# Four stacked graph layers on one core: layer 3 reordered, small VectorE steps moved, and the order of all chains from a table

## The chip, the cores and the metric

The kernel runs on one NeuronCore of a Trainium2 chip. The metric is the device time of one execution in microseconds (us). A core has engines that run side by side, each with its own queue that is worked off in order: PE (TensorE) multiplies 128x128 blocks and writes only to PSUM, DVE (VectorE) and POOL (GpSimd) do elementwise work, ACT (ScalarE) evaluates functions and copies, and SP (SyncE) issues DMAs between HBM and the on-chip memory SBUF. Engines wait for each other through semaphores. Three executions of the kernel before took 1044.95, 1046.66 and 1048.72 us; the median is 1046.66 us.

## The reference, cut to what matters

Inputs are x (32 batches of 512 nodes with 128 features, float32), one adjacency matrix adj (512x512, zeros and ones) and the weights. Every layer normalizes x over the features, takes the positive part, and adds the result of its own graph layer to x.

```
def layer(x, graph):
    h = maximum(layernorm(x), 0)
    return x + graph(h, adj)

# layer 0: h = x @ Wo;  u1 = h @ a1;  u2 = h @ a2
#   e = leaky(u1[idx1] + u2[idx2], 0.1)   (fixed pairs of nodes)
#   att = softmax(where(adj > 0, e, -9e15), over the FIRST index)
#   out = att @ h + x @ Ws
# layer 1: h = x @ Wp + bp;  s = leaky(src_i + dst_j, 0.2), softmax over j where adj > 0
#   h_gat = relu(layernorm((attn * adj) @ h))
#   z = relu(layernorm(((1 + eps) * h_gat + adj @ h_gat) @ W1 + b1))
#   out = relu(z @ W2 + b2 + h_gat)
# layer 2: Wh = h @ W;  e = leaky(f1_i + f2_j, 0.2), softmax over j where adj > 0
#   out = elu(att @ Wh + bias)
# layer 3: h0 = x @ W[0];  h1 = x @ W[1]
#   A = softmax over j of values drawn from e at the edges (the same for every batch)
#   out = (A * I) @ h0 + (A * (1 - I)) @ h1 + bias
```

Layer 3 needs, for each batch, the diagonal of A times h0 and the rest of A times h1. The product A x W can be multiplied in either order.

## The kernel before, in words

**Tiles.** A batch of 512 nodes is four chunks of 128 nodes on 128 partitions; a tile is 128x(4x128) float32. PSUM is eight banks of that size. Everything is float32; a 128x128 by 128x128 product is issued as two matmul passes.

**Preparation.** Once per execution, `prepare` and `prepare_last` load the weights and build what all batches share: `bias` (the mask, NEG where there is no edge), `adjT` (adj transposed), `biasT` (the mask transposed, first half, for layer 0), `edgeT` (0.2 times the mask transposed, for layer 2), `adjTe`, and for layer 3 `offT` (A without its diagonal, transposed) and `adiag_rep` (the diagonal, in every partition).

**One chain for each layer and batch** (`layer0` to `layer3`), 128 in all. Each begins with `preln`: VectorE takes mean and variance (L544, L546), 1/deviation comes from Ln and Exp on ScalarE (L560, L564) or from a power on GpSimd (L579), and the normalization itself runs on ScalarE for the first nine batches of layer 0 (L599) and on GpSimd otherwise (L614), four instructions of 128x128 each. Four transposes on TensorE (L454) put it into PSUM as `pt`, and ScalarE takes the positive part into `hT` (L624).

- Layer 0 projects `hT` with `w0_ext`, which has 128 weight columns and two score columns (L649), and copies the result out (L445). VectorE adds the two score columns (`sc`, L772) and takes the leaky ReLU (`ls`, L776); TensorE repeats `ls` along the free dimension (`prow`, L454). The scores of node pairs come from a matmul for the first nine batches (L749) and from small DMAs for the others (L759); `lt` is their leaky ReLU, on ScalarE for the first nine (L808) and on VectorE for the others (L801, L810). Then masked maxima (L791), exponentials (L848), and the products (L905 to L918).
- Layer 1 projects, adds a scalar to the scores (`src`, L939), attends (L672 to L726), squares the softmax sums for the layer norm (`q`, L950), multiplies by the adjacency (`pg`, L976: four blocks of 128x512), and runs a two-layer perceptron (L635).
- Layer 2 attends with rows and columns exchanged (L1021 to L1040); its mask is added by GpSimd (L1026).
- Layer 3 multiplies `hT` by the weights first (`p1`, L635: four 128x128 products), copies that to `h1` (L445), scales `pt` by the diagonal with the positive part taken (`own`, L1076), and for each of four output chunks accumulates `own` times W[0] (L1087) and four products of `offT` with `h1` (L1091). VectorE adds x and the bias (L1098) and SP writes the batch out.

**The order.** `Plan` writes the program's order by hand before anything runs. Every operation has an estimated length and a due time, `turn = begin + STRETCH * way`, where `begin` is that of its chain, `way` the length of the longest path to it within the chain, and STRETCH is 5.94. The begin of a chain is the sum of the gaps of the chains before it (GAPS, one for each layer; the first six gaps are widened by RAMP). The chains are listed with layer 1, 2 and 3 lagging layer 0 by 5, 11 and 16 batches (LAGS). The preparation has due times of its own (PREPARED, FILLED: a first one and a step). `run` then takes, again and again, the operation that could begin first on its engine by the estimates, and among those that could begin within SLACK of each other the one with the earliest due time, as long as its chain is among the WINDOW oldest unfinished ones and a tile is free. So an engine's queue is one fixed list; an operation whose input is late holds up all behind it on that engine. Where the plan sees TensorE idle for over 0.6 us, it puts in transposes that nobody reads (`idle`, L362). GpSimd operations are held by an added dependency behind VectorE operations that read through the same port.

Of the kernel before, what the change touches and what calls it, by code (L numbers as in the profile page):

```python
# [37 lines left out]
P = 128  # L38
NEG = -9.0e15
# [3 lines left out]
WINDOW = 24  # L43

OLD, KEPT = 1, 0
# [3 lines left out]
RESERVE = 1  # L49
# [13 lines left out]
SLACK = 0.112  # L63

STRETCH = 5.94

PREPARED, FILLED = (15.9, 2.63), (122.8, 2.7)

RAMP = 3.87
# [3 lines left out]
EARLY = 9  # L73

GAPS, LAGS = (2.58, 26.51, 19.83, 4.4), (0, 5, 11, 16)
# [32 lines left out]
class Operation:  # L108
    def __init__(self, engine, length, emit, chain, slots):
        self.engine, self.length, self.emit, self.chain, self.slots = engine, length, emit, chain, slots  # L110
        self.after, self.missing = [], 0
        self.ready = 0.0
        self.load, self.transfers, self.port = 0.0, 0, 0
        self.way = 0.0


class Plan:
# [4 lines left out]
    def __init__(self, tc):  # L122
        self.tc = tc
        self.ops = []
        self.chains = []
        self.begin = 0.0
        self.banks, self.idle_products = None, None

    def chain(self, gap=0.0, beside=None, name=""):


        self.chains.append([0, beside, self.begin, name])
        self.begin += gap

    def op(self, engine, length, emit, reads=(), writes=(), load=0.0, transfers=0, port=0):
# [3 lines left out]
        op.load, op.transfers, op.port = load, transfers, port  # L139
# [12 lines left out]
        for n in needs:  # L152
            n.after.append(op)
            if n.chain == k:
                op.way = max(op.way, n.way + n.length + DELAY[n.engine])
        count, beside, begin, _ = self.chains[k]
        turn = begin + STRETCH * op.way if beside is None else beside[0] + beside[1] * count
# [5 lines left out]
    def run(self):  # L163
# [18 lines left out]
        for _ in range(len(self.ops)):  # L182
# [59 lines left out]
            done = end + DELAY[op.engine]  # L242
# [39 lines left out]
def kernel(  # L282
# [36 lines left out]
    assert F == P and C == 4 and NE % P == 0 and AHEAD <= B <= 2 * HELD  # L319
# [35 lines left out]

# [38 lines left out]
    att = const("att", (P, 2))  # L394
# [11 lines left out]
    biasT = const("biasT", (P, C, N2))  # L406
# [11 lines left out]
    w0_ext = const("w0_ext", (P, P2))  # L418
# [40 lines left out]
    def score_weights(w, v_w, a_cols, v_a, cols, v_cols):  # L459
# [5 lines left out]
        op(PE, 0.15, lambda: nc.tensor.matmul(pc.t[:, 0, 0:2], lhsT=wT.t[:, 0, :], rhs=a_cols, start=True, stop=True),  # L465
           [wT, v_a], [pc])
        copy_op(DVE, 0.1, lambda: cols, lambda: pc.t[:, 0, 0:2], [pc], [v_cols])
# [6 lines left out]
    load(lambda: att, l0_att.rearrange("(t p) o -> p (t o)", p=P), [v_att])  # L474
# [6 lines left out]
    score_weights(lambda: wt_o.t[:, 0, :], wt_o, att, v_att, w0_ext[:, P:P2], v_w0)  # L481
# [26 lines left out]
    def no_edges():  # L508

        nc.vector.tensor_copy(cnt2T, counts.t[:, :, 1])  # L510
        nc.vector.tensor_scalar(maxbT, cnt2T, 0.0, NEG, ALU.is_le, ALU.mult)
# [6 lines left out]
    def mask_first():  # L518
        for jb in range(C):
            nc.vector.tensor_scalar(biasT[:, jb, :], adjT[:, jb, 0:N2], 0.0, NEG, ALU.is_le, ALU.mult)  # L520
# [63 lines left out]
    def preln(b, engine):  # L584
# [3 lines left out]
        rstd = inv_dev(mv, POOL if engine is ACT else ACT)  # L588
        shift = Value()
        xn = value(by_act if engine is ACT else by_pool, "xn")  # L590
        if engine is ACT:
# [5 lines left out]
            def norm():  # L597
                for c in range(C):
                    nc.scalar.activation(  # L599
                        xn.t[:, c, :], src[:, c, :], AF.Identity, bias=shift.own[:, c : c + 1],  # L600
# [21 lines left out]
        turn_op(lambda k: pt.t[:, k, :], lambda k: xn.t[:, k, :], [xn], [pt])  # L622
        hT = value(by_act, "hT")
# [16 lines left out]
    def project_scored(hT, w_ext, reads, first=0):  # L640

        h = parts(scored, "h", 2)
        for k in range(2):
            pt = value(banks, "proj")

            def emit(k=k, pt=pt):
                p = pt.t.rearrange("p (c t) f -> p c (t f)", c=2)[:, :, 0:P2]
# [5 lines left out]
                ACT, 0.26, lambda k=k: h[k].t[:, 2 * k : 2 * k + 2, first : first + P2],  # L653
                lambda pt=pt: pt.t.rearrange("p (c t) f -> p c (t f)", c=2)[:, :, 0:P2], [pt], [h[k]],
# [9 lines left out]
    def masked_max(prow, src, v_src, out, writes):  # L664

        rmax, top = Value(), [Value() for _ in range(C)]
        for ib in range(C):
# [9 lines left out]
            op(DVE, 0.61, emit, [prow, v_bias], [*writes(ib), top[ib]])  # L677
# [7 lines left out]
        def emit_nmax():  # L685
            nmax.own = small("nmax")
# [51 lines left out]
    def layer0(b):  # L738
        hT, _ = preln(b, ACT if b < EARLY else POOL)
        if b + AHEAD < B:  # L740
            load_x(b + AHEAD)
        h = project_scored(hT, w0_ext, [v_w0, v_w0b])
# [25 lines left out]
        sc, ls = Value(), Value()  # L768

        def emit_sc():  # L770
            sc.own = small("sc")
            nc.vector.tensor_add(sc.own, h[0].t[:, :, P], h[0].t[:, :, P + 1])  # L772

        def emit_ls():
            ls.own = small("ls")
            nc.vector.scalar_tensor_tensor(ls.own, sc.own, 0.1, sc.own, ALU.mult, ALU.max)  # L776

        dve(0.08, emit_sc, h, [sc], port=1)
        dve(0.08, emit_ls, [sc], [ls], port=1)
# [3 lines left out]
        for hf in range(H):  # L783

            def emit_max(hf=hf):
# [3 lines left out]
                for k in range(2):  # L789
                    jb = 2 * hf + k  # L790
                    nc.vector.tensor_tensor_reduce(  # L791
                        wide(y[hf].t)[:, k * N2 : k * N2 + N2], node[:, hf, :], biasT[:, jb, :], 1.0, LOWEST,
# [10 lines left out]
        def emit_lt():  # L803
            lt.own = small("lt", (P, 2, H))
            sums = u.sums.t[:, 0, 0:H] if early else lt1.own
            lt1_2 = sums.rearrange("p (o h) -> p o h", o=1).to_broadcast([P, 2, H])
            if early:
                nc.scalar.activation(lt.own, lt1_2, AF.Prelu, alpha=0.1)  # L808
                return
            nc.vector.scalar_tensor_tensor(lt.own, lt1_2, 0.1, lt1_2, ALU.mult, ALU.max)  # L810
# [13 lines left out]
        if early:  # L824
            op(ACT, 0.12, emit_lt, [u.sums], [lt])
        else:
            dve(0.08, emit_lt1, [u], [lt1], port=1)
            dve(0.08, emit_lt, [lt1], [lt], port=1)
# [103 lines left out]
    def layer1(b):  # L932
# [4 lines left out]
        def emit_src():  # L937
            src.own = small("src")
            nc.vector.tensor_add(src.own, h[0].t[:, :, P], score_p.to_broadcast([P, C]))  # L939

        dve(0.08, emit_src, [*h, v_score_p], [src], port=1)
# [6 lines left out]
        def emit_q():  # L948
            q.own = small("q")
            nc.vector.scalar_tensor_tensor(q.own, ssum[0].own, LN_EPS, ssum[0].own, ALU.mult, ALU.mult)  # L950
# [523 lines left out]
```

## Time and profile before

| | |
|---|---|
| three executions, median | 1046.66 us (1044.95 to 1048.72) |
| the profiled execution's own time | 1045.94 us |
| its span, first to last instruction | 1044.2 us |
| granted TensorE clock, mean | 0.998 |
| busy: TensorE matmul / weight load | 97% / 89% |
| busy: VectorE / ScalarE / GpSimd | 91% / 75% / 69% |
| TensorE passes / idle transposes among them | 8192 / 51 |

The page of the profile gives busy time for each engine (PE is the matmul, PEld the weight load that overlaps it), the span in 40 slices, the chain of work that ended last, and groups of instructions by source line with their count, busy time, mean duration and the idle time before them. Instructions of one engine overlap in their records: a matmul pass of 128 columns is on record for 275 ns, but passes of a stream start about 111 ns apart. The view by windows gives the busy time of each engine in a stretch of the span with the number of instructions, the timeline lists merged instructions by start, and the view of waits adds up who waited for whom.

The batches run through the layers like a pipeline: layer 0 of all batches is done after about 805 us of the span, layer 1 after about 925, layer 2 after about 1022; the first batch of layer 3 is added up (L1098) at 334 us and the last at 1040.

### The profile page before, as it was taken

How to read it: one execution, taken by the hardware profiler on the slowest of the kernel's cores; microseconds unless marked ns; L12 is line 12 of the kernel's file. 1: busy time of each engine (PE TensorE's matmuls, PEld its weight loads, DVE VectorE, ACT ScalarE, POOL GpSimd, SP SyncE). 2: the span in 40 equal slices, each digit the busy share in tenths (PEclk: the TensorE clock that was granted, in tenths of full speed). 3: DMA queues.
4: the chain of work that ended last, by engine and by line, in shares of the span. 5: the costliest groups of instructions: out<-in, count | busy, mean ns of one | idle time of the engine just before them, and what ended most of it. 6: DMA issues, size and time to landing. Idle time of an engine off the chain costs nothing.

```text
span 1044.2 us, 24575 instructions
## 1 busy us (share of the span) xinstructions
PE 1016.9 (97%) x8192; PEld 928.3 (89%) x8192; DVE 952.2 (91%) x3814; ACT 787.8 (75%) x2210; POOL 724.7 (69%) x962
## 2 busy tenths in 40 slices
PE   7999999999999999999999998999999999999998
PEld 6997888888899998989998898888989898899998
DVE  7999999999999999999999999999999988878862
ACT  7989787887887887777877776777777777766651
POOL 4563554786776767668767667767677677788992
PEclk9999999999999999999999999999999999999999
DMA  7300000000000000000000000000000000000011
GB/s 220 82 2 1 2 1 12 12 11 11 2 12 21 12 12 21 21 22 11 12 5 8 12 12 11 2 11 12 12 11 12 12 11 12 12 11 22 22 31 41
DMA packets 51726, 20.44 MB, mean 20 GB/s; under 512 B 16400, under 2 KB 51088, under 8 KB 51600
## 3 DMA queue, kind: packets, MB, share of 16 engines
q1 hardware_dynamic: 51600, 18.87, 6.9%
q8 instruction: 65, 1.06, 0.4%
q14 instruction: 61, 0.50, 0.2%
HBM read 10.43 MB, written 8.39 MB: 18 GB/s over the span
## 4 chain that ended last, share of the span: by engine, by line
PE 51%; DVE 36%; ACT 7%; POOL 4%; issue 2%; DMA 0%; SPq 0%; DVEq 0%; POOLq 0%; ACTq 0%
PE pt L454 7%; PE po L726 7%; PE pg L976 7%; PE po L1091 5%; DVE st L544 5%; PE po L1040 5%; DVE cols L1028 4%; PE proj L649 4%; PE prow L454 4%; DVE y L672 4%; DVE unused L672 3%; PE po L908 2%; DVE pT L721 2%; DVE mv L546 2%; DVE hn L964 2%; ACT y L705 2%
## 5 line engine op out<-in xcount | busy, mean ns | idle before, releaser
L614 POOL TENSOR_SCALAR xn<-xs,shift,rstd 128x128 f32<-128x128 f32 x476 | 232.6, 503 | 27.1 <-PE pt L454 19.4
L1026 POOL TENSOR_TENSOR cols<-cols,edgeT 128x512 f32<-128x512 f32 x128 | 161.4, 1278 | 69.5 <-ACT cols L1021 49.1
L1091 PE MATMUL po<-h,offT 128*128 128x128 f32 x1024 | 135.4, 275 | 0.5 <-ACT h L445 0.5
L976 PE MATMUL pg<-adjTe,hg 128*128 128x512 f32 x256 | 131.2, 595 | 1.0 <-ACT hg L971 0.9
L1091 PEld LDWEIGHTS po<-h,offT 128*128 128x128 f32 x1024 | 124.6, 192 | 0.7 <-ACT h L445 0.7
L1040 PE MATMUL po<-h,cols 128*128 128x129 f32 x1024 | 122.5, 275 | 0.0
L726 PE MATMUL po<-h,pT 128*128 128x128 f32 x1024 | 120.8, 275 | 0.1
L1040 PEld LDWEIGHTS po<-h,cols 128*128 128x128 f32 x1024 | 118.3, 192 | 0.7 <-issue 0.4
L726 PEld LDWEIGHTS po<-h,pT 128*128 128x128 f32 x1024 | 117.4, 192 | 0.7 <-ACT h L445 0.2
L544 DVE BATCH_NORM_STATS2 st<-xs 128x6 f32<-128x128 f32 x512 | 109.9, 276 | 6.7 <-POOL xs L1069 3.6
L649 PEld LDWEIGHTS proj<-w_ext,hT 128*128 128x128 f32 x768 | 94.9, 191 | 14.5 <-ACT hT L624 8.5
L649 PE MATMUL proj<-w_ext,hT 128*128 128x130 f32 x768 | 104.4, 277 | 2.5 <-ACT hT L624 2.0
L713 ACT ACTIVATE y<-y,nmax 128x512 f32<-128x512 f32 x128 | 90.7, 713 | 7.9 <-DVE nmax L687 4.7
L624 ACT ACTIVATE hT<-pt 128x512 f32<-128x512 f32 x128 | 74.7, 596 | 28.3 <-PE pt L454 19.8
L1030 ACT ACTIVATE cols<-cols 128x512 f32<-128x512 f32 x128 | 78.4, 634 | 22.2 <-DVE cols L1028 21.9
L1028 DVE TENSOR_TENSOR cols<-cols,prow 128x512 f32<-128x512 f32 x128 | 82.6, 678 | 13.7 <-PE prow L454 7.8
L672 DVE CUSTOM_DVE_ANT_0 unused<-prow,bias 128x512 bf16<-128x512 f32 x128 | 88.1, 688 | 6.3 <-PE prow L454 3.7
L705 ACT ACTIVATE y<-y,src 128x512 f32<-128x512 f32 x128 | 82.9, 712 | 13.6 <-DVE src L939 11.2
L721 DVE TENSOR_TENSOR pT<-pt,adjT 128x512 f32<-128x512 f32 x128 | 82.5, 683 | 9.6 <-PE pt L454 8.7
L1021 ACT ACTIVATE cols<-prow,h 128x512 f32<-128x512 f32 x128 | 80.1, 684 | 10.2 <-PE prow L454 10.1
L672 DVE CUSTOM_DVE_ANT_0 y<-prow,bias 128x512 f32<-128x512 f32 x128 | 82.2, 681 | 0.0
L454 PEld LDWEIGHTS pt<-ident,y 128*128 128x128 f32 x512 | 58.0, 141 | 26.5 <-ACT y L713 12.7
(219 smaller groups left out, 2618.3 us busy)
## 6 DMA issues: line engine op xcount, KB each, us to landing
xs<-in_x_dram SPq DMA_DIRECT2D x32, 256.0 KB, 4.2
out_dram<-yo SPq DMA_DIRECT2D x32, 256.0 KB, 2.3
u<-h SPq DMA_DIRECT2D x92, 0.5 KB, 1.8
bias<-in_adj_dram SPq DMA_DIRECT2D x4, 256.0 KB, 3.9
wts<-in_L_gnn_W_dram SPq DMA_DIRECT2D x3, 64.0 KB, 2.8
rows<-in_L_gnn_bias_dram SPq DMA_DIRECT2D x2, 64.0 KB, 5.7
wt_o<-L_gnn_others_weight_dram SPq DMA_DIRECT2D x1, 64.0 KB, 2.5
wts<-n_L_gnn_self_weight_dram SPq DMA_DIRECT2D x1, 64.0 KB, 3.9
```

The costliest lines, as they stand in the source:

```text
L454: nc.tensor.transpose(dst(k), src(k), ident)
L544: nc.vector.bn_stats(st[:, c, :], src(c))
L614: nc.gpsimd.tensor_scalar(xn.t[:, c, :], src[:, c, :], shift.own[:, c : c + 1], rstd.own[:, c : c + 1], ALU.add, ALU.mult,)
L649: nc.tensor.matmul(p[:, c, :], lhsT=column(hT, 2 * k + c), rhs=w_ext, start=True, stop=True)
L672: nc.vector.tensor_tensor_reduce(out(ib), wide(prow.t), bias[:, ib, :], 1.0, LOWEST, ALU.add, ALU.max, rmax.own[:, ib : ib + 1],)
L705: nc.scalar.activation(yw, yw, AF.Prelu, alpha=0.2, bias=src()[:, ib : ib + 1])
L726: nc.tensor.matmul(po[ib].t[:, ib, :], lhsT=pT.t[:, jb, :], rhs=h[0].t[:, jb, 0:P], start=(jb == 0), stop=(jb == C - 1),)
L976: nc.tensor.matmul(wide(pg.t), lhsT=hg.t[:, nb, :], rhs=adjTe[:, nb, :], start=(nb == 0), stop=(nb == C - 1))
L1026: op(POOL, 1.25, lambda jb=jb: nc.gpsimd.tensor_add(wide(pT[jb].t), wide(pT[jb].t), edgeT[:, jb, :]), [v_edgeT], [pT[jb]], port=1)
L1028: dve(0.6, lambda jb=jb: nc.vector.tensor_add(wide(pT[jb].t), wide(pT[jb].t), wide(max_row.t)), [max_row], [pT[jb]])
L1040: nc.tensor.matmul(half(ib // H)[:, ib % H, 0 : P + 1], lhsT=pT[jb].t[:, ib, :], rhs=h[0].t[:, jb, 0 : P + 1], start=(jb == 0), stop=(jb = ...
L1091: nc.tensor.matmul(po[ib].t[:, ib, :], lhsT=offT[:, jb, blk(ib)], rhs=h1.t[:, jb, :], start=False, stop=(jb == C - 1),)
```

## The change

1. **Layer 3.** `preln` gets `bent=True`: the normalization runs on ScalarE and takes the positive part there (Relu with scale and bias), so `xn` is final before the transposes and no `hT` is made. `pu` accumulates, over the four node chunks, `xn` times `offT` (four products with 512 columns each); ScalarE copies it to `uT`; then each output chunk is `own` times W[0] plus `uT` times W[1] (two 128x128 products). `own` becomes a plain multiplication. The shift of the normalization is made by VectorE instead of ScalarE.
2. **Small steps.** `w0_ext` gets a third score column, the sum of the other two, so `sc` is no longer computed; `ls` and `lt` are Prelu on ScalarE for all batches; `q` is a Square on ScalarE; `src` is a tensor_scalar with `score_p` as its scalar. The mask value becomes -2^53, `edgeT` is made with one multiplication by LEAKED, a fifth of it, and its first half takes the place of `biasT`.
3. **Layer 0.** Seven batches instead of nine are normalized on ScalarE (NORMED) and use the matmul for the pair sums (EARLY).
4. **Order.** The begin of each of the 128 chains stands in the table BEGINS; STRETCH has one value for each layer; LAGS, WINDOW, OLD, RESERVE, PREPARED and FILLED have other values; RAMP and GAPS are gone. The estimated length of the masked maximum is 0.65 instead of 0.61.

```diff
-NEG = -9.0e15
+NEG = -(2.0**53)
+LEAKED = NEG * 13421773 / 2.0**26
-WINDOW = 24
-OLD, KEPT = 1, 0
+WINDOW = 30
+OLD, KEPT = 8, 0
-RESERVE = 1
+RESERVE = 0
-SLACK = 0.112
-STRETCH = 5.94
-PREPARED, FILLED = (15.9, 2.63), (122.8, 2.7)
-RAMP = 3.87
+SLACK = 0.107
+STRETCH = (2.11, 4.99, 5.6, 10.21)
+PREPARED, FILLED = (109.918, 0.368), (137.184, 2.839)
-EARLY = 9
-GAPS, LAGS = (2.58, 26.51, 19.83, 4.4), (0, 5, 11, 16)
+EARLY = 7
+NORMED = 7
+LAGS = (0, 4, 10, 17)
+BEGINS = (
+    (
+        21.6, 15.9, 59, 42.6, 128.8, 162.9, 197.8, 222.6, 227.7, 120.1, 179.5, 208.9, 234.9, 301.8, 331.7, 360.3,
...
     def mask_first():
-            nc.vector.tensor_scalar(biasT[:, jb, :], adjT[:, jb, 0:N2], 0.0, NEG, ALU.is_le, ALU.mult)
+            nc.vector.tensor_scalar(edgeT[:, jb, 0:N2], adjT[:, jb, 0:N2], 0.0, LEAKED, ALU.is_le, ALU.mult)
...
-    def preln(b, engine):
+    def preln(b, engine, root=ACT, bent=False):
...
-        rstd = inv_dev(mv, POOL if engine is ACT else ACT)
+        rstd = inv_dev(mv, root)
...
-                        xn.t[:, c, :], src[:, c, :], AF.Identity, bias=shift.own[:, c : c + 1],
+                        xn.t[:, c, :], src[:, c, :], AF.Relu if bent else AF.Identity, bias=shift.own[:, c : c + 1],
...
+        if bent:
+            return xn, pt
         hT = value(by_act, "hT")
...
     def layer0(b):
-        hT, _ = preln(b, ACT if b < EARLY else POOL)
+        hT, _ = preln(b, *((ACT, POOL) if b < NORMED else (POOL, ACT)))
-        h = project_scored(hT, w0_ext, [v_w0, v_w0b])
+        h = project_scored(hT, w0_ext, [v_w0, v_w0b], 0, P2 + 1)
...
-            nc.vector.tensor_add(sc.own, h[0].t[:, :, P], h[0].t[:, :, P + 1])
-            nc.vector.scalar_tensor_tensor(ls.own, sc.own, 0.1, sc.own, ALU.mult, ALU.max)
+            nc.scalar.activation(ls.own, h[0].t[:, :, P2], AF.Prelu, alpha=0.1)
...
-            nc.vector.scalar_tensor_tensor(lt.own, lt1_2, 0.1, lt1_2, ALU.mult, ALU.max)
+            nc.scalar.activation(
+                lt.own, sums.rearrange("p (o h) -> p o h", o=1).to_broadcast([P, 2, H]), AF.Prelu, alpha=0.1
+            )
...
     def layer1(b):
-            nc.vector.tensor_add(src.own, h[0].t[:, :, P], score_p.to_broadcast([P, C]))
+            nc.vector.tensor_scalar(src.own, h[0].t[:, :, P], score_p, None, ALU.add)
...
-            nc.vector.scalar_tensor_tensor(q.own, ssum[0].own, LN_EPS, ssum[0].own, ALU.mult, ALU.mult)
+            nc.scalar.activation(q.own, ssum[0].own, AF.Square, scale=LN_EPS**0.5)
...
     def layer3(b):
-        hT, pt = preln(b, POOL)
+        xn, pt = preln(b, ACT, bent=True)
-        op(DVE, 0.6, lambda: nc.vector.scalar_tensor_tensor(wide(own.t), wide(pt.t), 0.0, adiag_rep, ALU.max, ALU.mult),
-           [pt, v_adiag_rep], [own])
+        op(DVE, 0.6, lambda: nc.vector.tensor_mul(wide(own.t), wide(pt.t), adiag_rep), [pt, v_adiag_rep], [own])
-        p1 = project(hT, wts[:, W_31, :], [v_wts[W_31]], "p1")
-        h1 = value(by_act, "h1")
-        copy_op(ACT, 0.49, lambda: h1.t, lambda: p1.t, [p1], [h1])
+        pu = value(banks, "pu")
+        for jb in range(C):
+            op(PE, 0.86, lambda jb=jb: nc.tensor.matmul(
+                wide(pu.t), lhsT=xn.t[:, jb, :], rhs=offT[:, jb, :], start=(jb == 0), stop=(jb == C - 1)),
+               [xn, v_offT], [pu])
+        uT = value(by_act, "uT")
+        copy_op(ACT, 0.49, lambda: wide(uT.t), lambda: wide(pu.t), [pu], [uT])
...
-                nc.tensor.matmul(
-                    po[ib].t[:, ib, :], lhsT=own.t[:, ib, :], rhs=wts[:, W_30, :], start=True, stop=False
-                )
-                for jb in range(C):
+                for k, (t, w) in enumerate(((own, W_30), (uT, W_31))):
                     nc.tensor.matmul(
-                        po[ib].t[:, ib, :], lhsT=offT[:, jb, blk(ib)], rhs=h1.t[:, jb, :],
-                        start=False, stop=(jb == C - 1),
+                        po[ib].t[:, ib, :], lhsT=t.t[:, ib, :], rhs=wts[:, w, :], start=(k == 0), stop=(k == 1)
                     )
...
-    order = []
     for n in range(B + LAGS[-1]):
-        for layer, gap, lag in zip((layer0, layer1, layer2, layer3), GAPS, LAGS):
+        for layer, begins, stretch, lag in zip((layer0, layer1, layer2, layer3), BEGINS, STRETCH, LAGS):
             if 0 <= n - lag < B:
-                order.append((layer, gap, n - lag))
-    for n, (layer, gap, b) in enumerate(order):
-        plan.chain(gap * RAMP if n < AHEAD else gap, name=layer.__name__)
-        layer(b)
+                plan.chain(begins[n - lag], stretch, name=layer.__name__)
+                layer(n - lag)
```

## The prediction, made before the changed kernel ran

> **What bounds the kernel now.** The page comes first. TensorE has passes on record for 97% of the span, VectorE 91%, ScalarE 75%, GpSimd 69%; TensorE and VectorE hold the chain that ended last.
>
> ```profile
> PE 1016.9 (97%) x8192; PEld 928.3 (89%) x8192; DVE 952.2 (91%) x3814; ACT 787.8 (75%) x2210; POOL 724.7 (69%) x962
> ...
> PE 51%; DVE 36%; ACT 7%; POOL 4%; issue 2%; DMA 0%; SPq 0%; DVEq 0%; POOLq 0%; ACTq 0%
> ```
>
> Second, the view by windows. Its columns are start:end, length, then busy time and instructions of PE, PEld, DVE, ACT and POOL, then the clock.
>
> ```profile
> 0.00:52.00 52.00, 45.36 (x381) 42.04 (x381) 44.12 (x255) 41.89 (x139) 26.41 (x48) 0.97 0.55 152
> 52.00:104.00 52.00, 49.85 (x400) 44.06 (x401) 51.44 (x259) 47.09 (x145) 28.32 (x44) 1.00 0.01 2
> 104.00:338.00 234.00, 230.59 (x1777) 204.50 (x1776) 231.44 (x966) 192.12 (x569) 157.55 (x210) 1.00 0.04 9
> 338.00:624.00 286.00, 282.96 (x2287) 259.14 (x2286) 270.32 (x1099) 222.09 (x628) 206.12 (x269) 1.00 0.06 14
> 624.00:754.00 130.00, 125.19 (x1012) 114.26 (x1012) 121.81 (x455) 96.31 (x273) 92.45 (x122) 1.00 0.04 10
> 754.00:988.00 234.00, 232.51 (x1900) 214.44 (x1900) 206.25 (x709) 168.69 (x418) 179.87 (x230) 1.00 0.05 14
> 988.00:1044.20 56.20, 50.44 (x448) 49.81 (x446) 26.77 (x78) 19.60 (x43) 34.01 (x43) 1.00 0.11 34
> ```
>
> From 52 to 338 us VectorE is as full as TensorE (51.44 + 231.44 of 286 us, 99%); after that TensorE alone is full, to the end.
>
> Third, the timeline of TensorE, because records overlap and a busy share hides short pauses. What a pass costs is the distance between starts.
>
> ```profile
> 505.42 1.02 PE L976 MATMUL pg<-adjTe,hg 128*128 128x512 f32 x2
> 506.28 0.60 PE L454 MATMUL pt<-ident,xn 128*128 128x128 f32 x4
> ...
> 511.27 0.39 PE L1087 MATMUL po<-wts,own 128*128 128x128 f32 x2
> 511.49 1.06 PE L1091 MATMUL po<-h,offT 128*128 128x128 f32 x8
> 512.38 0.39 PE L1087 MATMUL po<-wts,own 128*128 128x128 f32 x2
> ```
>
> Two 512-column passes take 0.86 us, 0.43 each; ten 128-column passes 512.38 - 511.27 = 1.11, 0.111 each. The groups by form list 7,424 passes of 128 to 130 columns for the batches (824 us at 0.111), 256 of 512 (110 us), 256 of L913 (four in 0.56 us, 36 us); the preparation and the pair sums make about 16. So TensorE has **986 us of work** in a span of 1044.2; 58 us are idle, of which the records show 27, and 8 more as transposes nobody reads. Summed by stage from the distances between starts, the idle time is 20.0, 5.8, 8.9, 5.2, 6.8, 4.4 and 6.7 us for the seven windows. Nothing can save more than the work it takes from TensorE plus a part of these 58.
>
> The Trainium skill ("Trainium Kernel Development and Optimization", Best Practices) says to judge the distance to the roofline by weight-load busy share and not by matmul busy share. Here that would be 89%, 116 us of room, twice what the starts leave: while a 512-column pass streams, the weight load is idle and TensorE is not. By that rule this forecast could lie as low as 930; the starts decide.
>
> **Part 1, layer 3 on TensorE.** Before: 8 + 8 + 32 = 48 passes of 128 columns, 48 x 0.111 = 5.33 us a batch. After: 8 passes of 512 columns and 16 of 128, 8 x 0.43 + 16 x 0.111 = 5.22. Saved 0.11 x 32 = 3.6 us. The multiplications are equally many; only the width differs. With the pair-sum matmuls of two batches gone (L749, 3.7 us for nine, so -0.8) and one more column in 256 projection passes (+0.2): **-4.2 us**, on the bounding engine, certain as far as the passes keep these rates.
>
> **Part 2, layer 3 elsewhere.**
>
> ```profile
> L614 POOL TENSOR_SCALAR xn<-xs,shift,rstd 128x128 f32<-128x128 f32 x476 | 232.6, 503 | 27.1 <-PE pt L454 19.4 <-ACT rstd L564 5.0 <-ACT cols L1030 2.0
> ...
> L624 ACT ACTIVATE hT<-pt 128x512 f32<-128x512 f32 x128 | 74.7, 596 | 28.3 <-PE pt L454 19.8 <-DVE own L1076 5.2 <-POOL xs L1069 1.1
> ...
> L599 ACT ACTIVATE xn<-xs,shift,rstd 128x128 f32<-128x128 f32 x36 | 14.7, 483 | 1.3 <-DVE shift L595 1.1 <-POOL xs L928 0.2
> ```
>
> The columns after the bar are busy us, mean ns, idle us before and its releasers. GpSimd loses 4 x 0.503 a batch, 64 us, and gets two batches of layer 0 back (+4, and -2 x 1.28 of powers): 69% becomes about 63%. ScalarE gets 4 x 0.483 = 1.93 a batch and loses hT (0.596) and the shift (L610, 0.199): +1.14 x 32 = 36 us. The copy of uT replaces that of h1 (0.584). The multiplication `own` from PSUM (L721 is the nearest: 0.683) replaces 0.682. VectorE gets 32 shifts at 0.170 (L595), 5 us. None of this is on the path by itself: after 338 us ScalarE is busy 507 of 706 us, 72%, and would be about 77%. If that cover failed, all 36 us could show. The new wait is normalization on shift: ScalarE makes 1/deviation, VectorE the shift, ScalarE waits for it, with exponentials and copies for TensorE queued behind. In the nine batches that already do so it waited 1.1 us in all, so 32 batches cost from 0 to 4 us of ScalarE; the far end is log waiting for the variances (L560 on DVE mv: 40.8 us in 37 waits, 1.1 each), 35 us. I take the near row, hidden by ScalarE's idle time. In the two batches of layer 0 that change sides, the pair sums become four DMAs each on SP's queue (92 to 100 of them, 1.8 us to landing, 32 loads and 32 stores beside them) and VectorE adds them up; masked maxima lie beside that landing, so nothing, or 2 x 1.8 if the plan put them early.
>
> **Part 3, small steps.**
>
> ```profile
> L939 DVE TENSOR_TENSOR src<-h,score_p 128x4 f32<-128x4 f32 x32 | 10.7, 336 | 0.0
> ...
> L772 DVE TENSOR_TENSOR sc<-h 128x4 f32<-128x4 f32 x32 | 8.3, 260 | 0.4 <-ACT h L445 0.3
> ...
> L776 DVE SCALAR_TENSOR_TENSOR ls<-sc 128x4 f32<-128x4 f32 x32 | 7.1, 221 | 0.0
> ```
>
> VectorE loses sc 8.3, ls 7.1, lt 4.7 (L810) and q 6.9 (L950), and about 5 of src's 10.7, if without a second tensor it falls to the shortest small steps (0.15): 32 us by records. By distances in the timeline (0.08 us for such a step, the median) it is 119 x 0.08 = 9.5. Less the shifts, VectorE is relieved of 5 to 27 us. ScalarE gets ls and lt (0.168, L808) and q (0.2 like L558): 16 us. Square is not in the trace; a table load is (one, 1.28 us), so q costs 32 x 0.2 if the function is in the loaded table, or up to 64 x 1.28 = 82 us more if not. I take the first: six functions already run from one load.
>
> The Trainium skill ("ScalarE: Activation LUTs", Rules for kernel authors) speaks against this part: relu, max, add and mul belong on VectorE, which is faster per element. With four elements the rows say the reverse: Prelu 0.168 on ScalarE, the same step 0.206 to 0.221 on VectorE. By the rule the part would be worth nothing or less, the sum 6.5 us longer.
>
> What it is worth: between 52 and 338 us, where VectorE is full, 13 batches of layer 0 and 12 of layer 1 pass; by the records 13 x 0.48 + 9 x 0.21 + 12 x 0.4 = 13 us go, by the distances 4. TensorE's idle time there is 14.7. I take the lower end, **-4 us**. Elsewhere, TensorE waits for VectorE's ls (4.8 us in 9 waits); sc and ls become one step on the engine that made the copy, so up to 4.8 goes, or nothing if ScalarE's queue is as late: **-2.5**.
>
> **Part 4, order.** The trace cannot show an order that has not run; it only bounds it by the idle time. From 0 to 52 us 20 us are idle: 3.9 before the first pass, the rest while few chains are under way; VectorE idles 7.9 there, and `edgeT` loses one multiplication a block and half the other (-2.6 us). Gain or loss up to 8; taken **-3**. From 624 to 754 the idle time is 6.8 us, at its neighbours' rate (5.2 in 286) it would be 2.4: 0 to -4.4, taken **-3**. The last 56 us: TensorE is full until 1039.4, and 4.8 us of adding and writing stay; taken **-1**. For loss, any stage can become like the first: the bound is what the plan misjudges, see the second rival.
>
> **Sum:** -4.2 - 4 - 2.5 - 3 - 3 - 1 = -17.7 us. The profiled execution took 1045.94 (1044.2 and 1.7 around it): 1028.2. The median is 0.7 above it: **1029 us**.
>
> **Rivals.**
> 1. Only the products count: the 58 us of idle time move but do not shrink, because work released on VectorE was beside TensorE anyway. For it: after 338 us TensorE idles only 23 of 706 us. Against: VectorE at 99% from 52 to 338. Time 1046.7 - 4.2 = 1042. Chance 0.15, a third of it within 0.3%.
> 2. Slower, through ScalarE's queue in layer 3: the 1.93 us of normalization, and the wait for its shift, stand before copies and exponentials that TensorE needs. For it: ScalarE was 91% busy from 52 to 104, and log already waits 40.8 us for VectorE. Against: 72% busy where layer 3 runs. It decides once TensorE loses over 17.7 / 32 = 0.55 us a batch; with half of the 1.93 exposed (31 us) the time is 1029 + 31 = 1060. Chance 0.16.
> 3. The change isn't what it says: Square brings table loads; 1029 + 82 = 1111. Chance 0.02.
> 4. The order halves the idle time (58 to 29): 1046.7 - 4.2 - 29 = 1013. Chance 0.05.
>
> The forecast itself (1015 to 1041) has 0.62. Beyond 0.3% (3 us, about what a measurement of this kernel can tell from no change) faster has 0.62 + 0.10 + 0.05 = 0.77, same 0.05, slower 0.18. The range 1014 to 1048 leaves out most of rivals 2 to 4, some 0.2.
>
> **What will show it.** Products: 256 passes of `pu` 0.43 apart and 512 of `po`. Relief: VectorE's busy time about 930, ScalarE's about 835, GpSimd's about 665. Order: TensorE's idle time by distances about 44 instead of 58, less in the first 52 us and from 624 to 754. Wrong would be: xn on ScalarE waiting for shift by more than 10 us in all with TensorE behind it, a second table load, or 512-column passes slower than 0.43.

## The result and the profile after

The changed kernel takes a median of **1052.22 us** (1049.47 to 1054.33, twelve executions); beside it, in the same rounds, the kernel before takes 1045.89 (1044.35 to 1048.72). The ratio is 1.0056, 95% interval [1.0043, 1.0069]: slower by 6 us, where 17.7 us of gain were forecast. The profiled execution took 1050.47 us, its span is 1048.8. Of all executions reported below one stands apart, 1283.8 us at a granted clock of 0.753 in experiment 16, where every other has 0.993 or more; the ratio of that experiment leaves it out.

The page of the kernel after, busy time by engine and the chain that ended last:

```profile
PE 1011.9 (96%) x7402; PEld 862.5 (82%) x7402; DVE 939.9 (90%) x3724; ACT 818.1 (78%) x2359; POOL 657.3 (63%) x838
...
PE 54%; DVE 21%; POOL 5%; ACT 5%; issue 2%; DVEq 0%; POOLq 0%; ACTq 0%
```

Every engine is busy for less time than before except ScalarE, and ScalarE is below its forecast (818 against 835). The relief took place; the time did not follow. The windows of the kernel after, columns as before:

```profile
0.00:52.00 52.00, 44.05 (x360) 40.18 (x361) 44.04 (x265) 40.32 (x138) 24.60 (x48) 1.00 0.54 152
52.00:104.00 52.00, 50.14 (x394) 44.38 (x393) 51.30 (x234) 46.00 (x161) 27.58 (x46) 1.00 0.03 7
104.00:338.00 234.00, 230.33 (x1788) 205.50 (x1787) 224.17 (x928) 200.38 (x606) 145.90 (x195) 1.00 0.03 5
338.00:624.00 286.00, 276.69 (x2014) 234.33 (x2013) 267.25 (x1044) 223.69 (x654) 184.71 (x232) 0.99 0.05 13
624.00:754.00 130.00, 125.76 (x927) 107.71 (x926) 120.61 (x451) 106.33 (x306) 90.36 (x120) 1.00 0.06 14
754.00:988.00 234.00, 228.18 (x1608) 189.21 (x1607) 207.06 (x737) 179.52 (x448) 161.48 (x184) 1.00 0.04 10
988.00:1048.80 60.80, 56.77 (x328) 41.18 (x326) 25.43 (x72) 21.86 (x49) 22.70 (x18) 1.00 0.16 48
```

The first number after the length is TensorE. From 338 to 624 us it fell from 282.96 to 276.69, from 754 to 988 from 232.51 to 228.18: the stages that were full before now have holes. (Layer 1, to which `src` belongs, ends in the kernel before at 982 us of the span, when L1003 writes its last batch back, and not at about 925 as said ahead.) By the distances between starts, TensorE's work fell from 986.3 to 982.3 us as forecast, but its idle time rose from 57.9 to 66.6:

| idle TensorE, us | 0-52 | 52-104 | 104-338 | 338-624 | 624-754 | 754-988 | to the end |
|---|---|---|---|---|---|---|---|
| before | 20.0 | 5.8 | 8.9 | 5.2 | 6.8 | 4.4 | 6.7 |
| after | 21.5 | 3.5 | 6.8 | 14.4 | 6.5 | 9.6 | 4.3 |

The groups of the kernel after, with different shapes kept apart (after the bar: busy us, mean ns; then idle us before them and the releasers):

```profile
L1090 PE MATMUL pu<-offT,xn 128*128 128x512 f32 x256 | 127.4, 599 | 0.0
...
L615 ACT ACTIVATE xn<-xs,shift,rstd 128x128 f32<-128x128 f32 x156 | 63.9, 485 | 6.3 <-DVE shift L611 2.8 <-DVE top L701 2.1 <-POOL xs L1078 0.6
...
L948 DVE TENSOR_SCALAR src<-h,score_p 128x4 f32<-128x4 f32 x32 | 26.0, 813 | 1.4 <-ACT h L460 1.3
...
L790 ACT ACTIVATE ls<-h 128x4 f32<-128x4 f32 x32 | 6.6, 207 | 0.1
...
L959 ACT ACTIVATE q<-ssum 128x4 f32<-128x4 f32 x32 | 6.3, 200 | 0.0
```

One line is out of place. `src` handles four elements in each partition, and each of its 32 instructions takes 813 ns on average, against 336 before. The short steps on ScalarE cost about what was estimated (`ls` 207 ns for 168, `q` 200 for 200). The timeline of the kernel after shows the longest `src` (columns: start, us, engine, line and operation; the bracket is the idle time before):

```profile
699.59 3.53 DVE L948 TENSOR_SCALAR src<-h,score_p 128x4 f32<-128x4 f32 x1
...
699.78 1.41 POOL L900 TENSOR_TENSOR hl<-hs,hl 128x256 fp32r<-128x256 f32 x2
...
701.16 0.72 POOL L937 TENSOR_TENSOR xs<-xs,rest 128x256 f32<-128x256 f32 x1
...
701.84 1.18 POOL L951 TENSOR_TENSOR h<-h,row_p 128x512 f32<-128x512 f32 x1
...
703.03 0.67 DVE L1037 TENSOR_TENSOR cols<-cols,prow 128x512 f32<-128x512 f32 x1
...
703.63 0.68 DVE L690 CUSTOM_DVE_ANT_0 y<-prow,bias 128x512 f32<-128x512 f32 x1
...
704.35 1.95 ACT L723 ACTIVATE y<-y,src 128x512 f32<-128x512 f32 x3 [3.20 <-DVE rmax L690]
...
706.30 1.35 PE L469 MATMUL pt<-ident,y 128*128 128x128 f32 x8 [2.76 <-ACT y L723]
```

Read it downwards. `src` begins at 699.59 and stays 3.53 us on VectorE while GpSimd goes from one instruction to the next (a run without a pause that began at 690.11). It ends at 703.12, just after the `h` of L951 has ended at 703.02. The masked maxima (L690) stand behind it in VectorE's queue, ScalarE's `y` waits 3.20 us for them, TensorE 2.76 us for `y`. Over the whole execution this wait of ScalarE's `y` is not much longer than before. There `y` waited for `src` itself or for the maxima, whichever came last, 13.6 us together; now it waits 17.9 us for the maxima (first two lines before, third after; us in total, times, longest):

```profile
ACT y L705 <- DVE src L939: 11.2, 12, 1.9
ACT y L705 <- DVE rmax L672: 2.4, 3, 1.2
ACT y L723 <- DVE rmax L690: 17.9, 17, 3.2
```

So the timeline shows one path by which a late `src` reaches TensorE. What all of them cost together has to come from experiments.

The reason is in a line of the change that the shortened diff above does not show and that the prediction did not weigh:

```diff
-        dve(0.08, emit_src, [*h, v_score_p], [src], port=1)
+        dve(0.08, emit_src, [*h, v_score_p], [src])
```

With `port=1` the plan keeps the operation apart from GpSimd operations that use the same port, as far as its estimated lengths hold, and makes GpSimd yield to it. Without it, `src` can be put beside any of them.

### The profile page after: what moved, and what is told of

It reads as the page before. It is cut to its first block, busy times and chain, and to the rows that moved or that the text cites. A ratio compares the mean times of both kernels' runs of the same rounds, so it can differ in the third digit from the quotient of the medians.

```text
span 1048.8 us, 22950 instructions
## 1 busy us (share of the span) xinstructions
PE 1011.9 (96%) x7402; PEld 862.5 (82%) x7402; DVE 939.9 (90%) x3724; ACT 818.1 (78%) x2359; POOL 657.3 (63%) x838
## 4 chain that ended last, share of the span: by engine, by line
PE 54%; DVE 21%; POOL 5%; ACT 5%; issue 2%; DVEq 0%; POOLq 0%; ACTq 0%
PE po L1049 8%; PE po L744 7%; PE pu L1090 7%; PE pt L469 6%; PE pg L985 5%; PE proj L667 4%; PE po L1100 4%; PE prow L469 3%; DVE unused L690 3%; DVE st L560 3%; PE po L917 2%; POOL xn L630 2%; DVE cols L1037 2%; DVE y L690 2%; ACT y L731 2%
## 5 line engine op out<-in xcount | busy, mean ns | idle before, releaser
L630 POOL TENSOR_SCALAR xn<-xs,shift,rstd 128x128 f32<-128x128 f32 x356 | 168.2, 488 | 65.6 <-PE pt L469 26.1
L985 PE MATMUL pg<-adjTe,hg 128*128 128x512 f32 x256 | 128.8, 594 | 0.0
L1090 PE MATMUL pu<-offT,xn 128*128 128x512 f32 x256 | 127.4, 599 | 0.0
L744 PE MATMUL po<-h,pT 128*128 128x128 f32 x1024 | 124.1, 275 | 0.9 <-DVE nltm L825 0.3
L667 PE MATMUL proj<-w_ext,hT 128*128 128x130 f32 (+1 forms) x768 | 106.0, 281 | 6.9 <-DVE rmax L690 2.8
L723 ACT ACTIVATE y<-y,src 128x512 f32<-128x512 f32 x128 | 86.2, 715 | 18.1 <-DVE rmax L690 17.9
L690 DVE CUSTOM_DVE_ANT_0 unused<-prow,bias 128x512 bf16<-128x512 f32 x128 | 88.0, 687 | 8.3 <-PE prow L469 4.8
L731 ACT ACTIVATE y<-y,nmax_a 128x512 f32<-128x512 f32 x128 | 90.9, 715 | 3.4 <-DVE nmax_a L705 3.2
L690 DVE CUSTOM_DVE_ANT_0 y<-prow,bias 128x512 f32<-128x512 f32 x128 | 82.5, 680 | 1.8 <-PE prow L469 1.0
L469 PEld LDWEIGHTS pt<-ident,xn 128*128 128x128 f32 x512 | 61.4, 142 | 23.9 <-issue 12.8
L460 ACT COPY h<-proj 128x260 f32<-128x260 f32 (+1 forms) x192 | 66.8, 375 | 17.8 <-PE proj L667 16.6
L469 PE MATMUL pt<-ident,xn 128*128 128x128 f32 x512 | 77.3, 275 | 1.2 <-POOL xn L630 0.8
```

What stands on the lines that cost most here:

```text
L469: nc.tensor.transpose(dst(k), src(k), ident)
L630: nc.gpsimd.tensor_scalar(xn.t[:, c, :], src[:, c, :], shift.own[:, c : c + 1], rstd.own[:, c : c + 1], ALU.add, ALU.mult,)
L667: nc.tensor.matmul(p[:, c, :], lhsT=column(hT, 2 * k + c), rhs=w_ext, start=True, stop=True)
L690: nc.vector.tensor_tensor_reduce(out(ib), wide(prow.t), bias[:, ib, :], 1.0, LOWEST, ALU.add, ALU.max, rmax.own[:, ib : ib + 1],)
L731: nc.scalar.activation(yw, yw, AF.Exp, bias=nmax.own[:, ib : ib + 1], accum_out=ssum[0].own[:, ib : ib + 1])
L744: nc.tensor.matmul(po[ib].t[:, ib, :], lhsT=pT.t[:, jb, :], rhs=h[0].t[:, jb, 0:P], start=(jb == 0), stop=(jb == C - 1),)
```

## The experiments

Theory (B in the expectations): `src`, no longer kept apart from GpSimd, waits through GpSimd's runs and holds the in-order queues behind it. Rivals: the new instruction form of `src` is slow by itself (A); the table of begins is a worse order (C); layer 3's new work on ScalarE is late. In the expectations, e10 stands for experiment 10, and so on.

**1. The form.** `src` as the tensor_tensor of before, order and port entry of the change.

```diff
-            nc.vector.tensor_scalar(src.own, h[0].t[:, :, P], score_p, None, ALU.add)
+            nc.vector.tensor_add(src.own, h[0].t[:, :, P], score_p.to_broadcast([P, C]))
```

> The changed kernel with src as the tensor_tensor of before; the plan is told the same as in the changed kernel, so every queue has the same order and one instruction a batch differs. Theory A (the tensor_scalar form itself waits out runs of GpSimd instructions, a tensor_tensor doesn't): src falls from 813 ns to about 340, TensorE loses some 8 us less behind it, time about 1044. Theory B (src is late because the order now puts it beside GpSimd instructions; the form doesn't matter): src stays near 800 ns, time stays near 1052. Theory C (src is beside the point, the table's order is worse): src may fall, the time stays within 2 us of 1052.

It takes 1049.12 us, ratio to the kernel before 1.0033 [1.0023, 1.0043]. The groups of this run:

```profile
L948 DVE TENSOR_TENSOR src<-h,score_p 128x4 f32<-128x4 f32 x32 | 24.8, 774 | 0.5 <-ACT h L460 0.2
```

The old form waits nearly as long as the new one (24.8 us for 26.0), and 3.1 of the 20 us go with it. The new form by itself is not it.

**2. A form that does not wait.** `src` as a reduction over one element, in the same place in every queue. It reads `h` alone and leaves out the addition of `score_p`.

```diff
-            nc.vector.tensor_scalar(src.own, h[0].t[:, :, P], score_p, None, ALU.add)
+            nc.vector.tensor_reduce(src.own, h[0].t[:, :, P : P + 1], AX.X, ALU.add)
```

> The changed kernel with the same order; src is a reduction over one element, which reads one tensor at one element a cycle; it leaves out the addition of the scalar score_p. Theories A and B: src about 160 ns, 20 us less on VectorE, time about 1043 to 1045. Theory C: time within 2 us of 1052.

It takes 1031.27 us, ratio 0.9857 [0.9842, 0.9873].

```profile
L948 DVE TENSOR_REDUCE src<-h 128x4 f32<-128x4 f32 x32 | 4.7, 145 | 1.5 <-ACT h L460 1.4
```

21.3 us of `src` on VectorE are gone and 20.9 of the kernel's time, nearly one for one. The expectation had the direction right and the price wrong: it gave 1043 to 1045. The wait of `y` for the maxima falls with it:

```profile
ACT y L723 <- DVE rmax L690: 8.2, 11, 2.0
```

Here 24 of the 32 `src` run wholly beside a busy GpSimd and none takes more than 0.16 us. In the kernel after, all of the 18 that take over 0.4 us lie beside GpSimd instructions that cover 95% of them or more, up to five in a row; the four with no GpSimd work beside them take 0.19 to 0.22.

**3. The form in the kernel before,** its `port=1` and order kept (the first edit the other way round).

> The kernel before with src as tensor_scalar and its order kept (the plan still holds it apart from GpSimd). Theory A: src rises from 336 to 600 ns or more, time 1049 or more. Theory B and C: src stays at 340 or falls to 160, time 1046 within 1.5 us.

It takes 1047.54 us, ratio 1.0015 [1.0005, 1.0025], with `src` at 336 ns as before. If the form costs anything, it is 1.6 us, not 20. The shortest `src` did get longer: beside no GpSimd work it takes 0.195 to 0.224 us here, 0.130 to 0.156 in the kernel before.

**4. The whole work, with the old rules of order** (GAPS, RAMP, STRETCH, LAGS, WINDOW and the rest as before; no table), alone and **5.** with the reduction.

```diff
-        for layer, begins, stretch, lag in zip((layer0, layer1, layer2, layer3), BEGINS, STRETCH, LAGS):
+        for layer, gap, lag in zip((layer0, layer1, layer2, layer3), GAPS, LAGS):
```

> All the work of the changed kernel (layer 3, small steps, seven early batches), but the order by the old rules: gaps, one stretch, old lags, window and slack. src is tensor_scalar and not held apart. Theory C: faster than the kernel before, by the 4 us of TensorE work and more, 1036 to 1042. Theories A and B: src is late here too (600 ns or more), time 1046 to 1053.

> All the work of the changed kernel by the old order rules, as before, with src as a reduction over one element (the scalar score_p is left out). It asks what src's wait costs in another order. If the price is the same everywhere (about 1 us of span for 1 us of VectorE, as the table's order showed): src goes from 20.1 to 4.7 us, the time from 1033.8 to 1018 or 1020. If the table's order is what makes a late src expensive: 1030 to 1034.

They take 1033.78 us, ratio 0.988 [0.9863, 0.9898], and 1025.09 us, 0.9792 [0.9776, 0.9809]. In this order `src` takes 627 ns on average, 1.53 us at most; freeing 15.2 us of VectorE (20.1 to 4.9) brings 8.7. Both expectations missed: `src` is late in the fourth as theories A and B said, but the time lies 12 us below their range, and the fifth lies between its two ranges. A wait for GpSimd has another price in another order.

**6.** `src` on ScalarE, in the table's order, and **7.** in the old rules' order. The computation is complete in both.

```diff
-            nc.vector.tensor_scalar(src.own, h[0].t[:, :, P], score_p, None, ALU.add)
+            nc.scalar.activation(src.own, h[0].t[:, :, P], AF.Identity, bias=score_p)
```

> The changed kernel in its own order, src complete, but as an activation on ScalarE (Identity with score_p as bias) in the place where the plan has it on VectorE. If the wait for the port is the whole loss, this keeps the gain of the reduction and pays 32 x 0.2 us of ScalarE that has room: 1030 to 1035. If the gain of the reduction came from leaving the addition out, or ScalarE's queue matters as much: 1045 or more.

> The same on the old order rules: all the work of the changed kernel, src on ScalarE in VectorE's place. With one price everywhere 1020 to 1023, below both kernels by 2%; with the price bound to the table's order 1031 to 1035.

They take 1031.72 us, ratio 0.9854 [0.9837, 0.9871], as expected, and **1024.62 us, 0.9791 [0.9774, 0.9808]**, between the two ranges given. The windows of the seventh:

```profile
104.00:338.00 234.00, 228.28 (x1737) 200.47 (x1735) 224.97 (x919) 198.12 (x594) 150.49 (x190) 1.00 0.04 7
338.00:624.00 286.00, 285.51 (x2114) 244.85 (x2113) 265.08 (x1080) 247.08 (x714) 185.63 (x242) 1.00 0.06 15
624.00:754.00 130.00, 130.00 (x956) 110.89 (x955) 119.20 (x466) 108.47 (x307) 88.28 (x118) 1.00 0.04 10
754.00:988.00 234.00, 234.00 (x1659) 194.43 (x1659) 204.69 (x704) 178.31 (x451) 160.79 (x179) 1.00 0.05 15
```

and of the sixth, in the same stages:

```profile
104.00:338.00 234.00, 232.62 (x1805) 208.04 (x1804) 220.65 (x924) 206.73 (x633) 144.74 (x195) 1.00 0.03 5
338.00:624.00 286.00, 281.17 (x2046) 239.65 (x2045) 267.02 (x1069) 229.87 (x676) 195.90 (x249) 0.99 0.06 14
624.00:754.00 130.00, 128.58 (x970) 112.36 (x969) 121.73 (x442) 107.99 (x308) 89.18 (x113) 1.00 0.05 12
754.00:988.00 234.00, 230.08 (x1612) 190.12 (x1611) 203.68 (x726) 181.90 (x456) 166.80 (x183) 1.00 0.05 14
```

From 338 us on TensorE is on record for 649.5 of these 650 us with the old rules, with the table for 639.8; from 104 to 338 the table is ahead, 232.62 for 228.28. The instructions are the same but for eight idle transposes. In all the table loses 7.1 us here.

The three medians make the sum of the change: all its work in the old order, with `src` on ScalarE, 1045.89 to 1024.62 (-21.3); the table instead of the rules, to 1031.72 (+7.1); `src` back on VectorE beside GpSimd, to 1052.22 (+20.5). Taken the other way round, `src` on VectorE beside GpSimd costs 9.2 with the old rules (1024.62 to 1033.78), and the table then 18.4 (to 1052.22). Together the two cost 27.6 us, where each alone costs 7.1 and 9.2.

**8 to 10. Layer 3 in the kernel before:** all of it; the normalization on ScalarE alone; attention first alone, with the normalization left on GpSimd and a Relu on ScalarE ahead of the transposes.

```diff
-        hT, pt = preln(b, POOL)
+        hT, pt = preln(b, ACT)
```

(this is the ninth; the tenth makes `pu` and `uT` as the change does)

> The kernel before with the new layer 3 alone (normalization with the positive part on ScalarE, attention first), its own small steps and order rules. By the prediction's terms: TensorE's work 3.6 us less, GpSimd 64 us less, ScalarE 36 us more, hidden: 1038 to 1043. If ScalarE's queue becomes late (the second rival): 1050 or more. If GpSimd's relief itself is worth something, because VectorE waits less for the port it shares: 1036 or less.

> The kernel before with one thing moved: layer 3 is normalized on ScalarE instead of GpSimd; the weights are still multiplied first and hT is still made. Layer 3 alone gave -16.8 us where the products explain -3.6. If GpSimd's relief (64 us less of it) is the rest: 1032 to 1036. If the rest comes from the shorter product chain or from the order that the plan happens to find: 1042 or more.

> The kernel before with the other half: attention and x are multiplied first, but the normalization stays on GpSimd; ScalarE takes the positive part from SBUF to SBUF ahead of the transposes, in place of hT. GpSimd, VectorE and ScalarE have the work of before, TensorE 3.6 us less. If GpSimd's relief is the rest: 1041 to 1045. If the shorter chain (no projection and copy between the positive part and the big product) is: 1036 or less.

In this order they take 1029.98 us, ratio 0.9843 [0.9826, 0.9859]; 1043.27, 0.9978 [0.9969, 0.9987]; and 1028.64, 0.9838 [0.9823, 0.9854]. The eighth fell where GpSimd's relief would have put it, but the ninth, which has that relief without the new order of products, gains 2.5 us. Attention first alone brings 17.2 us, where 3.6 were counted for its products. TensorE's work falls by those 3.6, its idle time by 12.8 (57.9 to 45.1).

**11. `port=1` given back,** the rest of the change as it is. The plan then lays out another order.

> The changed kernel with the mend that first comes to mind: the plan is told again that src reads through the shared port, and holds it apart from GpSimd. The table of begins stays. If only src's place matters: src back to 0.2 to 0.35 us and 1031 to 1035, as with src on ScalarE. If the table holds only for the very order it was made with, the new order loses more than src gave: 1050 to 1075.

It takes 1064.12 us, ratio 1.0178 [1.0163, 1.0192]: the obvious mend makes it worse.

```profile
L948 DVE TENSOR_SCALAR src<-h,score_p 128x4 f32<-128x4 f32 x32 | 8.8, 277 | 0.0
```

`src` is cured, and yet TensorE idles 78.7 us. The numbers in the table fit one plan; a small change of the plan's rules makes another order with the same begins, and that one is bad. So `port=1` does keep `src` short, but that leaving it out was a mistake for the time is not shown.

**12 to 15. How much is the order alone?** One gap shifted, in the kernel before and in the tenth: the first from 2.58 to 2.5, or the last from 4.4 to 4.8.

```diff
-GAPS, LAGS = (2.58, 26.51, 19.83, 4.4), (0, 5, 11, 16)
+GAPS, LAGS = (2.5, 26.51, 19.83, 4.4), (0, 5, 11, 16)
```

> The kernel before with nothing changed but one number of its order rules: layer 0's gap 2.50 instead of 2.58. The same instructions in another order. If the order alone can move the time as much as the parts of this change do: more than 6 us off 1046, either way. If not: 1043 to 1049.

> Attention first alone (e10) with the same gap 2.50. If the 17 us of e10 belong to the product order, it is 14 us or more below e12; if 13 of them were a lucky order, it is 4 us below, or anything.

> The kernel before with layer 3's gap 4.8 instead of 4.4, nothing else. Same question as for the gap of layer 0: 1043 to 1049 if the order hardly matters, over 6 us off if it does.

> Attention first alone with layer 3's gap 4.8. 14 us or more below e14 if the gain belongs to the product order; about 4 us below if only TensorE's work counts.

| order | weights first | attention first | difference |
|---|---|---|---|
| as before | 1045.89 | 1028.64 | -17.2 |
| first gap 2.5 | 1061.28, 1.0148 [1.0133, 1.0164] | 1038.80, 0.9935 [0.9922, 0.9947] | -22.5 |
| last gap 4.8 | 1044.16, 0.9981 [0.9972, 0.999] | 1041.02, 0.9954 [0.9941, 0.9968] | -3.1 |

A gap shifted by 0.08 us costs 15 us with none of the work changed. Attention first gains in all three orders, but between 3 and 22 us. The second row meets the expectation for a gain that belongs to the work, the third the one for TensorE's passes alone: how much of the 17.2 is the work and how much the order cannot be told from these runs.

**16 and 17. Rules fitted anew** for the whole work with `src` on ScalarE, and the plan told so; two sets of numbers.

```diff
-GAPS, LAGS = (2.58, 26.51, 19.83, 4.4), (0, 5, 11, 16)
+GAPS, LAGS = (2.48, 22.05, 24.39, 4.4), (0, 5, 12, 16)
...
-        dve(0.08, emit_src, [*h, v_score_p], [src])
+        op(ACT, 0.2, emit_src, [*h, v_score_p], [src])
```

> All the work of the changed kernel by the old order rules, src on ScalarE and told to the plan as such, with gaps 2.48, 22.05, 24.39, 4.4, lags 5, 12, 16 and small shifts of slack, ramp and the preparation's due times. Same work as e7 (1024.6), another order. If orders of this work scatter as the four shifted ones did: 1015 to 1040. A time below 1024 would be the fastest version here.

> The same with gaps 2.28, 26.51, 18.87, 4.65, old lags, slack 0.133. Same work again, a third order: 1015 to 1040.

They take **1021.69 us, ratio 0.9766 [0.9751, 0.978]**, the fastest of all, and 1024.72, 0.9796 [0.9782, 0.981]. TensorE idles 36 us in the first of them. Three sets of rules thus give 1021.7 to 1024.7, the table 1031.7.

## Why the prediction was wrong, by its own steps

**The step that failed is Part 3's term for `src`.** The prediction put `src` down as "about 5 of src's 10.7" saved, "if without a second tensor it falls to the shortest small steps (0.15)". It rose to 26.0 us. Two things were missed. The duration of 336 ns in the groups was a mean over two kinds: 18 of the 32 took 0.13 to 0.17 us, 15 of these with no GpSimd work beside them; the other 14 took 0.25 to 1.28, and GpSimd instructions cover 95% of each or more. A mean so far above the shortest step was the sign of a wait, not of the work. And the change dropped the protection against that wait, an argument in the plan's entry and not in the instruction. The 0.15 was not to be had either: without GpSimd beside it this form takes 0.19 us or more (experiment 3). That it is this wait is shown: with the same queues, a form that does not wait (experiment 2) and another engine (6) both give 1031 to 1032 us. Rival 2 had the path right (a late step in an in-order queue, TensorE behind it) but the wrong engine: the wait of `xn` for its shift came to 2.8 us in three waits, inside the 0 to 4 given.

**Part 4's terms for the order have the wrong sign.** They are -7 together. With `src` out of the way the table costs 7.1 us against the old rules (experiments 6 and 7), and 7 to 10 against the fitted ones. Neither error alone leaves the range of 1014 to 1048: the table without the wait takes 1031.72, the wait with the old rules 1033.78. Only both together give 1052.22.

The other terms:

- **TensorE's work, -4.2:** measured -4.0. `pu` passes start 0.43 us apart (two from 580.97 to 581.83 in TensorE's timeline).
- **Layer 3 elsewhere, taken as hidden:** GpSimd 657 (about 665 forecast). ScalarE rose by 30 us to 818, not by 47 to 835, and its cover held. But the term was mis-sized for the gain: attention first alone takes 12.8 us from TensorE's idle time in the order of before, beside the 3.6, though with the last gap at 4.8 the two together bring only 3.1. The normalization's move by itself is worth 2.5. "Hidden" meant only that nothing gets worse; that the new chain could let others come earlier was not priced. That it does so because it is shorter is not shown.
- **Small steps from 52 to 338 us, -4:** idle there fell from 14.7 to 10.3, and to 6.3 with `src` on ScalarE. But with the old rules it stays at about 15 (experiment 7), so that the small steps bring it is not shown. **The hop of `ls`, -2.5:** TensorE's idle time before the repeat of `ls` went from 5.2 to 0.0, and to 0.2 in experiment 7; how much of it the span gained was not measured. One table load served Square, Prelu and all others, so rival 3 is out.
- **Order by stage, -3, -3 and -1.** The first 52 us: 21.5 for 20.0 idle, no gain (19.8 in experiment 6). From 624 to 754: 6.5 for 6.8, but 2.6 with `src` out of the way, and none with the old rules, so that it does not need the table. The end: 4.3 for 6.7, -2.4, but about 4 with the old rules too. What the bound by idle time left open came: against experiment 7, with the same instructions, experiment 6 idles 8.1 us for 0.9 from 338 to 624 and 7.2 for none from 754 to 988, and gets back only 3.3 for 11.0 from 104 to 338. The prediction said that an order which has not run cannot be read from the trace, and then took only its gains.
- **The sum:** without the wait of `src`, -14.2 (experiment 6) for -17.7. That the two are near each other is luck: it is -21.3 of work where the terms had -10.7, and +7.1 of order where they had -7.

**What stays open.** Why the table's order loses 7 to 10 us against three sets of rules was seen only as holes from 338 us on, not traced to one decision of the plan. How much attention first is worth apart from the order lies between 3 and 22 us. Whether the form of `src` costs the 1.6 us of experiment 3 or the 3 of experiment 1 is near what the runs can tell. An order laid out with the lengths of the trace was not tried, nor the whole work by the old rules with `port=1` kept, nor a GpSimd that yields in the table's order without a new plan.

## What to carry to other kernels

Where a tiny instruction's mean duration is twice the shortest of its kind, look at its single executions and at what the other engines do during each: it may be waiting, as here, and a change may take away what keeps the wait short. Read the plan's entries in a diff (ports, dependencies, reserves) as closely as the instructions, since one dropped argument let in a wait that costs 20 us in the order that ran, as much as all the work of the change brings in another (21). And a static order is a part of the measurement: compare two versions of the work in more than one order, because one gap shifted by 0.08 us moved this kernel by 15 us.

## What the runs showed of the hardware

A VectorE instruction of 128x4 that adds `score_p`, tensor_tensor or tensor_scalar alike, stood for up to 3.52 and 3.53 us beside GpSimd instructions that followed each other without a pause; a reduction of the same four elements (0.16 at most), and the same sum on ScalarE (299 ns), did not. Whether the second operand or the form makes the difference, the runs do not show. In the longest case it passed over four ends of GpSimd instructions (699.81, 700.51, 701.19 and 701.88) and got in at the fifth (703.02), though GpSimd went on there too; what decides at which end it gets in, the runs do not show.

The Trainium skill ("SBUF — State Buffer", SBUF: two separate sides) describes the port that VectorE and GpSimd share as a lock that whoever starts first holds for the whole instruction. The wait agrees with it in kind; its length here was up to five instructions, not one. An estimate by that rule, with the port going to VectorE at the first end, is the rest of one `xn`, 0.22 us (699.59 to 699.81), where 3.53 was measured.

The share of weight loads fell from 89% to 82% in the kernel after and to 84% in the seventh experiment, of which one is slower and the other faster than before. It did not follow the time; TensorE's idle time by the distances between starts did (57.9 us before, 66.6 after, about 40 in the seventh).
